# Token order written by ScalarE, a shared kernel mixing, a later gate and a rearranged end in a four-layer vision network on one Trainium2 core

## The chip, the cores and the metric

The kernel runs on one NeuronCore of a Trainium2 chip. The metric is the device time of one execution in microseconds (us). Engines are named as in the profile: PE is TensorE's matmul and PEld its weight load, DVE is VectorE, ACT is ScalarE, POOL is GpSimd, SP is SyncE, which here only issues DMAs. Everything is computed in fp32.

## What is computed

The input is three maps of 256 channels and 48 x 48 pixels. Four layers follow one another; each adds a function of the group-normalised map to the map:

```python
# x: (3, 256, 48, 48); _gn: group norm, 32 groups, no affine part
x = x + layer0(_gn(x))       # 1x1 convolutions and two attention and MLP blocks
x = x + layer1(_gn(x))       # 3x3 convolution, kernel mixed from 8 experts for each map
x = x + layer2(_gn(x))       # plain 3x3 convolution and bias
x = x + layer3(_gn(x))       # Mamba (state-space) block over 2304 tokens of a map

# layer1: the mixed kernel of each map
routing = sigmoid(mean_over_pixels(x) @ routing_ws)             # (3, 8)
ws = einsum('ne,eoihw->noihw', routing, weight)                 # weight (8, 256, 256, 3, 3)

# layer3: tokens in row order, 512 inner channels, 16 states
xn = layer_norm(tokens); x_in, z = split(xn @ in_proj)
u = silu(causal_conv4(x_in)); dt, B, C = projections of u
h = exp(dt * A) * h + dt * B * u            # for each token, channel and state
y = sum over states of h * C + u * D
out = (y * silu(z)) @ out_proj
```

## The kernel before

A map stays in SBUF as 128 partitions (channels) by 2 channel halves (ct) by 2304 pixels. The maps are processed in the order 2, 1, 0. Layer 0 takes the span up to about 1590 us; the change touches there only the count of softmax sums outside a safe range (L841, L842). That count is a product with ones on PE and a copy to `flag`; a flag above zero starts an exact version of the whole network afterwards, which does not happen with this input.

**Layers one and two** are 3x3 convolutions by a one-dimensional fast algorithm along the rows: four neighbouring columns become six transformed columns. So a map lies in four *phases*: pixel (j, n) is column j of group n of four, all n of phase 0 first. Each layer has a *unit* for each map, six units in all; a unit has two halves h of the rows, a half two halves m of the output channels, and these have six products (`products`, L1356) of six matmuls with 288 columns each, which go through five PSUM buffers. ACT copies some of them to SBUF (L1372), DVE turns six products into four phases and adds them to the map. ACT pads the next half (L310) into `xpad`, a pool of one buffer, from which DVE makes the transformed columns `vt`; the moments for the next group norm (`moments`, L1400 and L1407, then PE's group sum L184 and DVE's L186) also use `xpad` for their discarded outputs.

The kernels of the units are made beside other units, by generators that are advanced 13 steps after each output half. `mixed(b)` reads 48 pieces of 128 x 768 (8 experts, 2 ct, 3 taps dx), 384 KB each, and adds each, scaled by its routing weight, to a sum `u`: the first expert on ACT (L273), the others by one DVE operation (L275). Then DVE transforms the sum from three taps to six (L256 to L261), one ct after the other. `mixed(1)` runs beside unit 0 and is needed by unit 1, `mixed(0)` beside unit 1 for unit 2; `mixed(2)` was made earlier. The order of instructions in these units is the scheduler's.

When a unit of layer two is complete, 18 DMAs in all (six for each map, L1460) write the map to the DRAM tensor `xd` in chunks of 384 tokens, phase by phase, in runs of 384 bytes. SP issues those of maps 2 and 1, ACT's queue those of map 0. Beside units 4 and 5, `early_preparation` computes the first steps of layer three for the first chunks.

**Layer three** goes through 18 chunks of 384 tokens (6 for each map). A chunk has 4 blocks m of 128 inner channels, and a block 2 steps (h = 0 and 1) of 8 states; so 8 steps a chunk, 144 in all. A step has 8 parts: one scan on DVE (L1572) with the decays that ACT has made by an exponential in PSUM (L1564, three slots). Before a step its inputs are filled, half by DVE (L1535) and half by POOL (L1539, from `dtur`); after it POOL multiplies the states by C (`times_c`, L1580), and PE adds the states of the step before up in one PSUM tile `ps_y` (`add_states`: a product with D, L1592, and 8 products, L1597; the pool has one buffer). `gate` (L1604) is a DVE product of `ps_y` with the silu of z. A table gives the other work of a chunk to a step's parts, in places MID, LATE and PE_: normalisation and projections of the next chunk, output projection (`project_y`, L1198 and L1202) and store of the last one. All engines' orders are written out by hand there (`keep_order`).

Two stages turn phases into tokens: `group_scale` (L1057) reads the fetched chunk by phases and writes it with a stride of four elements; and `project_y` adds the map to the output with an identity product (L1202) whose input is read with that stride (`in_order`). At the end of the program, behind the last scan, come POOL's `times_c` of the last step, `add_states`, `gate`, and both output projections with their stores.

Of the kernel before, what the change touches and what calls it, by code (L numbers as in the profile page):

```python
# [16 lines left out]
P = 128  # L17
B = 3
# [65 lines left out]
def net(  # L84
# [68 lines left out]

    xd = [dram.tile([P, NCH, CT, CH], F32, name=f"xd{b}", bufs=1) for b in range(B)]
    norm3 = {}
# [106 lines left out]

    def mixed(b, pool):

        u = weights[b] = pool.tile([P, 6, 3, CT, 256], F32, name="u")
        for e in range(EXPERTS):
            for ct in range(CT):
                for dx in range(3):
                    wt = part_of_kernel(we[e], ct, dx)
                    re = route[b][:, e : e + 1]  # L270
                    dst = u[:, dx, :, ct, :]
                    if e == 0:
                        nc.scalar.activation(dst, wt, AF.Copy, scale=re)  # L273
                    else:
                        nc.vector.scalar_tensor_tensor(dst, wt, re, dst, ALU.mult, ALU.add)  # L275
                    yield
        for ct in range(CT):
            kernel_transform(u, ct)
            yield
# [80 lines left out]
    with ExitStack() as l0:  # L360
# [147 lines left out]
        with ExitStack() as p2:  # L508
# [323 lines left out]
            if not exact:  # L832

                ext = small.tile([P, 2], F32, name="ext")
                nc.vector.tensor_reduce(ext[:, 0:1], sums, AX.X, ALU.max)
                nc.vector.tensor_reduce(ext[:, 1:2], sums, AX.X, ALU.min)
                nc.vector.tensor_scalar(ext[:, 0:1], ext[:, 0:1], 1.0 / SUM_MIN, None, ALU.is_gt)
                nc.vector.tensor_scalar(ext[:, 1:2], ext[:, 1:2], 1.0 / SUM_MAX, None, ALU.is_lt)
                nc.vector.tensor_tensor(ext[:, 0:1], ext[:, 0:1], ext[:, 1:2], ALU.add)
                pe = one()  # L840
                nc.tensor.matmul(pe[:1, :1], ext[:, 0:1], ones[:, 0:1], start=True, stop=True)  # L841
                nc.vector.tensor_copy(flag, pe[:1, :1])  # L842

# [95 lines left out]
        for steps in small_steps:  # L939
            at_once(steps)  # L940

    psg = ctx.enter_context(tc.tile_pool(name="psg", bufs=1, space=PSUM))
    rooms, w3v, chunks = {}, {}, {}

# [17 lines left out]
    def w3_rooms():  # L965
# [10 lines left out]
        halves = [t.rearrange("p (t n) -> p t n", t=2) for t in pieces]  # L976
        for name, got in zip(("xp", "xg", "sq", "ot"), (halves[:1], halves[1:2], halves[2:3], halves[3:5])):
            rooms[name] = got
# [54 lines left out]
    def fetch(at):  # L1033
        k = chunks[at] = Chunk()
        k.at = at
        k.b, k.c = todo[at]
        k.before = chunks.get(at - 1)
        k.xp = room(k, "xp")
        nc.sync.dma_start(k.xp, xd[k.b][:, k.c])

# [7 lines left out]

    def in_order(t):

        return t.rearrange("p (j n) -> p n j", j=4)

    def group_scale(k):
        sc, sh = norm3[k.b]
        k.xg = room(k, "xg")
        for ct in range(CT):
            nc.scalar.activation(  # L1057
                k.xg[:, ct, :].rearrange("p (n j) -> p j n", j=4),
                k.xp[:, ct, :].rearrange("p (j n) -> p j n", j=4), AF.Identity,
                bias=sh[:, ct : ct + 1], scale=sc[:, ct : ct + 1],  # L1060
            )
# [133 lines left out]

    def project_y(k, mo):
        for m in range(DI):
            nc.tensor.matmul(  # L1198
                bank[mo], w("out", m * 256 + mo * P, P), k.sz[:, m, :],
                start=m == 0, stop=False,  # L1200
            )
        nc.tensor.matmul(bank[mo], ident, in_order(k.ot[:, mo, :]), start=False, stop=True)  # L1202

    def residual(k):
        k.ot = room(k, "ot")
        nc.sync.dma_start(k.ot, xd[k.b][:, k.c])

# [64 lines left out]
    def early_preparation():  # L1272

        exp_ln_tables()
        fetch(0)
        winx, cwb = x2_rooms()
# [42 lines left out]
        k = chunks[0]  # L1319
        while 1 not in norm3:  # L1320
            yield
# [24 lines left out]
    with ExitStack() as l1:  # L1346
# [42 lines left out]
        units = [(layer, b) for layer in range(2) for b in ORDER]  # L1389
        beside = {0: mixed(1, upools[1]), 1: mixed(0, upools[0]), 2: plain(upools[1])}  # L1390
        halves = [(k, h) for k in range(len(units)) for h in range(2)]
# [21 lines left out]
        def next_norm(layer, b):  # L1413

            last = layer and b == ORDER[-1]
            known = None if last else moments(b)
            for _ in range(5):
                yield
            _, sc, sh = yield from group_norm_steps(b, pss, "s", known=known)
            if layer == 0:  # L1420
                norms[b] = sixth(sc, sh)
            else:
                keep = const.tile([P, 2, CT], F32, name=f"norm3{b}")
                nc.vector.tensor_copy(keep[:, 0, :], sc)
                nc.vector.tensor_copy(keep[:, 1, :], sh)
                norm3[b] = keep[:, 0, :], keep[:, 1, :]
# [8 lines left out]
        def between():  # L1435
            next(pending, None)
            if at_unit >= 4:
                next(early, None)

        vt = first_v  # L1440
        pending = iter(())
        for n, (k, h) in enumerate(halves):
# [7 lines left out]
            for m in range(2):  # L1450
                output(b, h, m, u, vt, v("l2_bias", 0, 2) if layer else None)
                for _ in range(13):
                    next(beside.get(k, iter(())), None)
            vt = ahead
            if layer and h == 1:
                phases = xs[b].rearrange("p t (j n) -> p (t j) n", j=4)

                queue = nc.sync if k + 1 < len(units) else nc.scalar
                for c in range(NCH):
                    queue.dma_start(  # L1460
                        xd[b][:, c].rearrange("p t (j n) -> p (t j) n", j=4),
                        phases[:, :, c * (CH // 4) : (c + 1) * (CH // 4)],
                    )
            if h == 1:
                for _ in pending:
                    pass
                pending = next_norm(layer, b)
                next(pending)
        for _ in pending:
            pass  # L1470
# [9 lines left out]
    with ExitStack() as l3:  # L1480
# [95 lines left out]
        def times_c(s):  # L1576
            at, m, h = steps[s]
            cb = chunks[at].bc[1][:, 2 * h : 2 * h + 2, :].unsqueeze(2)
            hc = scn.tile([P, 2, 4, CH], F32, name="hc")
            nc.gpsimd.tensor_tensor(  # L1580
                hc, tiles[s][:, :, :, 1:], cb.broadcast_to([P, 2, 4, CH]), ALU.mult
# [33 lines left out]
        for s, (at, m, h) in enumerate(steps):  # L1615
            if m == 0 and h == 1 and at + 2 <= last:
                fetch(at + 2)
            for part in range(8):
# [5 lines left out]
                if part % 4 == 1:  # L1624
                    if h == 1 and part == 5 and s >= 3:
                        gate(*steps[s - 3][:2])
                    run(at, j, MID)
                if part % 4 == 3:
                    run(at, j, LATE)
# [16 lines left out]
            if h == 0 and s + 2 < len(steps):  # L1646
                spread_pe(chunks[steps[s + 2][0]], steps[s + 2][1])
        end = len(steps) - 1
        add_states(end)
        gate(*steps[end][:2])  # L1650
        k = chunks[last]
        residual(k)
        for mo in range(2):
            project_y(k, mo)
            store(k, mo)
# [114 lines left out]
```

## Time and profile before

| | us |
|---|---|
| median of 3 runs | 3594.66 (3594.13 to 3596.95) |
| profiled execution, its own time | 3598.05 |
| its span in the profile | 3596.3 |
| units 0 and 1 of the convolutions (1592 to 1774) | 182 |
| unit 2 and layer two (1774 to about 2098) | 324 |
| first scan of layer three | at 2107.64 |
| last scan of layer three ends | at 3570.93 |

Busy time of the whole span: PE 3179.0 us (88%), DVE 3003.0 (84%), ACT 2333.6 (65%), POOL 1440.4 (40%, nearly all of it in layer three). The granted clock was 0.934 in the mean. In the profile a row of the groups gives engine, operation, output and inputs, shapes, how many, then busy time and mean ns of one, then the idle time just before them and what ended it. A product of 128x384 on PE is two records in fp32, one behind the other. In a timeline the columns are start, duration, engine, line, operation, and in brackets the idle time before it and who ended it.

### The profile page before, as it was taken

To read this page: it belongs to the slowest core of one execution; us is meant where nothing else is said; L and a number is where in the kernel's file an instruction comes from. 1 tells how busy PE (TensorE), PEld (TensorE's weight loads), DVE (VectorE), ACT (ScalarE), POOL (GpSimd) and SP (SyncE) were. 2 spreads that over 40 slices of the span, in tenths; PEclk is the share of its full clock that TensorE was granted. 3 is DMA by queue.
4 is the path that set the end of the run, shared out by engine and by line. 5 is a ranking of instruction groups with operands and counts; after the bars stand their busy time and mean duration, and the time that the engine had idled before them with its cause. 6 is when DMAs were issued, how large, how long until landed. Compare 5 with 4: busy or idle time off the path is not lost. (4 is left out here: it accounts for less than half of the span.)

```text
span 3596.3 us, 45582 instructions
## 1 busy us (share of the span) xinstructions
PE 3179.0 (88%) x17154; PEld 1438.0 (40%) x17154; DVE 3003.0 (84%) x3304; ACT 2333.6 (65%) x3477; POOL 1440.4 (40%) x386
## 2 busy tenths in 40 slices
PE   7999999999999999977899987888888888788875
PEld 4323232352322324546677743333333333333331
DVE  4798989959989896479965379999999999999996
ACT  2788787748877875332123447777777777777774
POOL 0000000000000000210000059999999999999998
PEclk9999999999999999988999988889999999888986
DMA  4000000000000001756402234444444444444441
GB/s 181 3 1 1 1 2 1 1 40 1 1 1 1 2 1 60 243 171 219 164 28 58 60 75 116 102 112 106 111 98 111 102 108 101 118 106 107 107 106 36
DMA packets 170648, 266.50 MB, mean 74 GB/s; under 512 B 42849, under 2 KB 137633, under 8 KB 168498
## 3 DMA queue, kind: packets, MB, share of 16 engines
q1 hardware_dynamic: 152082, 243.44, 25.2%
q10 hardware_dynamic: 18336, 20.06, 1.7%
q8 instruction: 136, 2.23, 0.3%
q14 instruction: 94, 0.77, 0.1%
HBM read 216.31 MB, written 46.89 MB: 73 GB/s over the span
## 5 line engine op out<-in xcount | busy, mean ns | idle before, releaser
L610 ACT ACTIVATE pt<-ps_s 128x1024 f32<-128x1024 f32 x972 | 939.0, 1022 | 236.9 <-PE ps_s L606 219.3
L1572 DVE TENSOR_TENSOR_SCAN hs<-ps_da,hs 128x385 f32<-128x385 f32 x1152 | 1012.8, 939 | 63.2 <-ACT ps_da L1564 45.4
L686 DVE TENSOR_TENSOR part<-part,pt 128x2048 f32<-128x2048 f32 x396 | 906.5, 2289 | 79.4 <-ACT pt L610 54.8
L1564 ACT ACTIVATE ps_da<-dtr,u 128x384 f32<-128x384 f32 x1152 | 658.0, 582 | 311.1 <-DVE hs L1572 292.6
L162 POOL TENSOR_TENSOR rstd<-ve,mhalf 128x2 f32<-128x2 f32 (+1 forms) x26 | 17.9, 691 | 1529.1 <-DVE ve L160 1529.1
L606 PE MATMUL ps_s<-q,kt 32*128 32x512 f32 (+1 forms) x4320 | 615.2, 593 | 2.3 <-DVE q L567 0.9
L619 PE MATMUL acc<-pt,vt 128*32 128x512 f32 (+1 forms) x4320 | 522.3, 562 | 8.1 <-DVE o L666 8.0
L1356 PE MATMUL ps_c<-vt,u 128*128 128x288 f32 x1728 | 430.0, 410 | 45.7 <-DVE u L261 45.7
L1580 POOL TENSOR_TENSOR hc<-hs,x 128x3072 f32<-128x3072 f32 x72 | 445.6, 6188 | 37.8 <-PE ps_g L1155 13.4
L1580 POOL TENSOR_TENSOR hc<-hs,bc 128x3072 f32<-128x3072 f32 x72 | 444.1, 6169 | 37.7 <-DVE hs L1572 14.1
L1109 PE MATMUL ps_g<-u 128*128 128x384 f32 x1152 | 389.2, 493 | 3.1 <-ACT u L1118 3.1
L1356 PEld LDWEIGHTS ps_c<-vt,u 128*128 128x128 f32 x1728 | 330.3, 192 | 140.1 <-issue 34.8
L606 PEld LDWEIGHTS ps_s<-q,kt 32*128 32x128 f32 x4320 | 220.0, 183 | 388.5 <-issue 227.1
L1109 PEld LDWEIGHTS ps_g<-u 128*128 128x128 f32 x1152 | 215.0, 190 | 174.5 <-issue 14.0
L1597 PE MATMUL ps_y<-hc,u 128*32 128x384 f32 x2304 | 246.1, 550 | 30.7 <-POOL hc L1580 27.4
L1539 POOL TENSOR_TENSOR hs<-dtur,x 128x1536 f32<-128x1536 f32 x72 | 247.9, 3443 | 17.4 <-DMA dtur<-dtud 8.8
L1539 POOL TENSOR_TENSOR hs<-dtur,bc 128x1536 f32<-128x1536 f32 x72 | 248.5, 3451 | 6.5 <-ACT ps_g L1087 2.4
L619 PEld LDWEIGHTS acc<-pt,vt 128*32 128x32 f32 x4320 | 95.7, 108 | 363.8 <-issue 328.1
L1155 PE MATMUL ps_g<-wconv,u 17*128 17x384 f32 x144 | 79.2, 684 | 97.2 <-ACT x L1176 97.2
L1372 ACT COPY cb<-ps_c 128x288 f32<-128x288 f32 x48 | 19.0, 396 | 219.1 <-PE ps_c L1356 200.7
L1067 PE MATMUL ps_g<-wconv,u 128*128 128x384 f32 x144 | 87.5, 780 | 67.0 <-ACT x L1176 66.6
L1597 PEld LDWEIGHTS ps_y<-hc,u 128*32 128x32 f32 x2304 | 64.6, 118 | 201.9 <-issue 151.0
(236 smaller groups left out, 3517.1 us busy)
## 6 DMA issues: line engine op xcount, KB each, us to landing
wconv<-in_we SPq DMA_DIRECT2D x144, 384.0 KB, 4.3
dtr<-dtd SPq DMA_DIRECT2D x288, 192.0 KB, 3.8
dtur<-dtud SPq DMA_DIRECT2D x288, 96.0 KB, 4.1
wconv<-xd SPq DMA_DIRECT2D x36, 384.0 KB, 4.4
x<-bcd SPq DMA_DIRECT2D x72, 192.0 KB, 5.8
dtd<-x SPq DMA_DIRECT2D x36, 384.0 KB, 2.4
bc<-bcd SPq DMA_DIRECT2D x72, 192.0 KB, 5.5
yc<-ycat ACTq DMA_DIRECT2D x18, 576.0 KB, 4.7
```

What stands on the lines that cost most here:

```text
L606: nc.tensor.matmul(s[:, j, cols], kt[r, mt * P : (mt + 1) * P], q[r, :n], start=True, stop=True,)
L610: nc.scalar.activation(p[:, h0 : h0 + 2, :], s, AF.Exp)
L619: nc.tensor.matmul(acc[h * HD : (h + 1) * HD, :n], vt[:, mt, g * P + h * HD : g * P + (h + 1) * HD], p[:, h, cols], start=mt == 0, stop=mt ...
L686: nc.vector.tensor_tensor(part, first_p if group == 1 else part, p, ALU.add)
L1067: nc.tensor.matmul(bank[to], w3v["less"][:, int(to != ct), :], k.xg[:, ct, :], start=ct == 0, stop=ct == CT - 1,)
L1109: nc.tensor.matmul(bank[m % 2], w3v["wtap"][:, tap, ct, m * P : (m + 1) * P], k.xn[:, ct, tap : tap + CH], start=tap == 0 and ct == 0, sto ...
L1356: nc.tensor.matmul(pc[:, :HN], u[:, i, dy, ct, m * P : (m + 1) * P], vt[:, i, ct, dy * TW : dy * TW + HN], start=ct == 0 and dy == 0, stop ...
L1539: nc.gpsimd.tensor_tensor(hs[:, :, 2:4, 1:], k.rows[m][1].unsqueeze(1).broadcast_to([P, 2, 2, CH]), bb, ALU.mult,)
L1564: nc.scalar.activation(slots[n % 3][:, 1 : CH + 1], chunks[at].rows[m][0][:, q, :], AF.Exp, scale=amat[:, col : col + 1],)
L1572: nc.vector.tensor_tensor_scan(b, slots[(8 * s + part) % 3][:, : CH + 1], b, 0.0, ALU.mult, ALU.add)
L1580: nc.gpsimd.tensor_tensor(hc, tiles[s][:, :, :, 1:], cb.broadcast_to([P, 2, 4, CH]), ALU.mult)
L1597: nc.tensor.matmul(k.y_ps[32 * q : 32 * q + 32, :CH], fold, hc[:, g, q, :], start=False, stop=h == 1 and g == 1,)
```

## The change

1. *Token order.* `xd` becomes 2304 tokens in order for each channel half. `store_tokens` lets ACT write half a map in token order (12 copies of 128x1152 in all, with a stride of four elements) into an `xpad` buffer, or for the last half into a `vt` buffer, and one DMA of 1.18 MB stores it; it is called in the middle of the half that follows. `group_scale` then works in place on contiguous tokens, `project_y`'s identity product reads contiguously and comes first. `early_preparation` waits for the stores it reads, and `next_norm` yields nine times in place of five.
2. *Kernel mixing.* In `mixed(1)` and `mixed(0)` one piece of the six of each expert (second ct, third dx) is no longer added by ACT and DVE: ACT writes the routing weight times the identity into `each`, PE multiplies the piece with it in two products of 384 columns, which add up over the experts in two PSUM banks, and after the last expert ACT copies the sums to `u` in four pieces.
3. *Gate.* `gate` stands behind part 7's scan and no longer behind part 5's.
4. *Count.* The product with ones and the copy to `flag` are issued behind the small steps of the convolution part.
5. *End.* The last step's `times_c` is two DVE products of 128x1536; the identity products and three of the four products of each output projection stand before the last `add_states`.

```diff
@@ -151,7 +151,7 @@
     ycat = [dram.tile([P, 3, N], F32, name=f"ycat{b}", bufs=1) for b in range(B)]
-    xd = [dram.tile([P, NCH, CT, CH], F32, name=f"xd{b}", bufs=1) for b in range(B)]
+    xd = [dram.tile([P, CT, N], F32, name=f"xd{b}", bufs=1) for b in range(B)]
     norm3 = {}
@@ -260,7 +260,10 @@
...
         nc.vector.tensor_tensor(g1, t, g1, ALU.add)
-    def mixed(b, pool):
+    def mixed(b, pool, shared=False):
         u = weights[b] = pool.tile([P, 6, 3, CT, 256], F32, name="u")
@@ -269,7 +272,23 @@
...
                     dst = u[:, dx, :, ct, :]
-                    if e == 0:
+                    if shared and ct == CT - 1 and dx == 2:
+                        flat = wt.rearrange("p y o -> p (y o)")
+                        each = tmp.tile([P, P], F32, name="each")
+                        nc.scalar.activation(each, ident, AF.Copy, scale=re)
+                        for j in range(2):
+                            nc.tensor.matmul(
+                                bank[j], each, flat[:, j * 384 : (j + 1) * 384],
+                                start=e == 0, stop=e == EXPERTS - 1,
+                            )
+                        if e == EXPERTS - 1:
+                            for y, o, n in ((0, 0, 256), (1, 0, 128), (1, 128, 128), (2, 0, 256)):
+                                at = y * 256 + o
+                                j = at // 384
+                                nc.scalar.copy(
+                                    dst[:, y, o : o + n], bank[j][:, at - 384 * j : at - 384 * j + n]
+                                )
+                    elif e == 0:
                         nc.scalar.activation(dst, wt, AF.Copy, scale=re)
@@ -837,9 +856,6 @@
...
                 nc.vector.tensor_tensor(ext[:, 0:1], ext[:, 0:1], ext[:, 1:2], ALU.add)
-                pe = one()
-                nc.tensor.matmul(pe[:1, :1], ext[:, 0:1], ones[:, 0:1], start=True, stop=True)
-                nc.vector.tensor_copy(flag, pe[:1, :1])
         early.close()
@@ -938,12 +954,16 @@
...
             at_once(steps)
+        if not exact:
+            pe = one()
+            nc.tensor.matmul(pe[:1, :1], ext[:, 0:1], ones[:, 0:1], start=True, stop=True)
+            nc.vector.tensor_copy(flag, pe[:1, :1])
     psg = ctx.enter_context(tc.tile_pool(name="psg", bufs=1, space=PSUM))
-    rooms, w3v, chunks = {}, {}, {}
+    rooms, w3v, chunks, stored = {}, {}, {}, set()
     def room(k, name):
@@ -974,7 +994,7 @@
...
         halves = [t.rearrange("p (t n) -> p t n", t=2) for t in pieces]
-        for name, got in zip(("xp", "xg", "sq", "ot"), (halves[:1], halves[1:2], halves[2:3], halves[3:5])):
+        for name, got in zip(("xg", "sq", "ot"), (halves[:2], halves[2:3], halves[3:5])):
             rooms[name] = got
@@ -1035,8 +1055,8 @@
...
         k.before = chunks.get(at - 1)
-        k.xp = room(k, "xp")
-        nc.sync.dma_start(k.xp, xd[k.b][:, k.c])
+        k.xg = room(k, "xg")
+        nc.sync.dma_start(k.xg, xd[k.b][:, :, k.c * CH : (k.c + 1) * CH])
     class Chunk:
@@ -1046,17 +1066,11 @@
-    def in_order(t):
-        return t.rearrange("p (j n) -> p n j", j=4)
     def group_scale(k):
         sc, sh = norm3[k.b]
-        k.xg = room(k, "xg")
         for ct in range(CT):
             nc.scalar.activation(
-                k.xg[:, ct, :].rearrange("p (n j) -> p j n", j=4),
-                k.xp[:, ct, :].rearrange("p (j n) -> p j n", j=4), AF.Identity,
+                k.xg[:, ct, :], k.xg[:, ct, :], AF.Identity,
                 bias=sh[:, ct : ct + 1], scale=sc[:, ct : ct + 1],
@@ -1193,17 +1207,18 @@
...
         nc.scalar.copy(k.sz[:, m, :], bank[j])
-    def project_y(k, mo):
-        for m in range(DI):
+    def project_y(k, mo, lo=0, hi=DI):
+        if lo == 0:
+            nc.tensor.matmul(bank[mo], ident, k.ot[:, mo, :], start=True, stop=False)
+        for m in range(lo, hi):
             nc.tensor.matmul(
                 bank[mo], w("out", m * 256 + mo * P, P), k.sz[:, m, :],
-                start=m == 0, stop=False,
+                start=False, stop=m == DI - 1,
             )
-        nc.tensor.matmul(bank[mo], ident, in_order(k.ot[:, mo, :]), start=False, stop=True)
     def residual(k):
         k.ot = room(k, "ot")
-        nc.sync.dma_start(k.ot, xd[k.b][:, k.c])
+        nc.sync.dma_start(k.ot, xd[k.b][:, :, k.c * CH : (k.c + 1) * CH])
     def store(k, mo):
@@ -1272,6 +1287,8 @@
...
         exp_ln_tables()
+        while (2, 1) not in stored:
+            yield
         fetch(0)
@@ -1317,7 +1334,7 @@
...
         k = chunks[0]
-        while 1 not in norm3:
+        while 1 not in norm3 or (1, 1) not in stored:
             yield
@@ -1387,7 +1404,7 @@
         units = [(layer, b) for layer in range(2) for b in ORDER]
-        beside = {0: mixed(1, upools[1]), 1: mixed(0, upools[0]), 2: plain(upools[1])}
+        beside = {0: mixed(1, upools[1], True), 1: mixed(0, upools[0], True), 2: plain(upools[1])}
         halves = [(k, h) for k in range(len(units)) for h in range(2)]
@@ -1414,7 +1431,7 @@
...
             known = None if last else moments(b)
-            for _ in range(5):
+            for _ in range(9):
                 yield
@@ -1437,8 +1454,30 @@
...
                 next(early, None)
+        def store_tokens(b, h):
+            last = (b, h) == (ORDER[-1], 1)
+            if last:
+                t = vp.tile([P, 6, CT, (HR + 2) * TW], F32, name="vt")
+                t = t.rearrange("p i t n -> p (i t n)")
+            else:
+                t = pad.tile([P, 4, CT * (HR + 2) * PW + 2], F32, name="xpad")
+                t = t.rearrange("p j n -> p (j n)")
+            t = t[:, : CT * 4 * HN].rearrange("p (t n) -> p t n", t=CT)
+            for ct in range(CT):
+                nc.scalar.copy(
+                    t[:, ct, :].rearrange("p (n j) -> p j n", j=4),
+                    xs[b][:, ct, :].rearrange("p (j n) -> p j n", j=4)[
+                        :, :, h * HN : (h + 1) * HN
+                    ],
+                )
+            queue = nc.scalar if last else nc.sync
+            queue.dma_start(xd[b][:, :, h * 4 * HN : (h + 1) * 4 * HN], t)
+            stored.add((b, h))
         vt = first_v
-        pending = iter(())
+        behind, pending = None, iter(())
         for n, (k, h) in enumerate(halves):
@@ -1451,21 +1490,18 @@
...
                     next(beside.get(k, iter(())), None)
+                if m == 0 and behind is not None:
+                    store_tokens(*behind)
+                    behind = None
             vt = ahead
-            if layer and h == 1:
-                phases = xs[b].rearrange("p t (j n) -> p (t j) n", j=4)
-                queue = nc.sync if k + 1 < len(units) else nc.scalar
-                for c in range(NCH):
-                    queue.dma_start(
-                        xd[b][:, c].rearrange("p t (j n) -> p (t j) n", j=4),
-                        phases[:, :, c * (CH // 4) : (c + 1) * (CH // 4)],
-                    )
+            if layer:
+                behind = b, h
             if h == 1:
...
                 next(pending)
+        store_tokens(*behind)
         for _ in pending:
@@ -1577,6 +1613,15 @@
...
             hc = scn.tile([P, 2, 4, CH], F32, name="hc")
+            if s == len(steps) - 1:
+                for g in range(2):
+                    nc.vector.tensor_tensor(
+                        hc[:, g], tiles[s][:, g, :, 1:],
+                        cb[:, g].broadcast_to([P, 4, CH]), ALU.mult,
+                    )
+                tiles[s] = hc
+                return
             nc.gpsimd.tensor_tensor(
@@ -1622,9 +1667,9 @@
...
                 if part % 4 == 1:
-                    if h == 1 and part == 5 and s >= 3:
-                        gate(*steps[s - 3][:2])
                     run(at, j, MID)
+                if h == 1 and part == 7 and s >= 3:
+                    gate(*steps[s - 3][:2])
                 if part % 4 == 3:
@@ -1645,13 +1690,16 @@
...
         end = len(steps) - 1
-        add_states(end)
-        gate(*steps[end][:2])
         k = chunks[last]
...
         for mo in range(2):
-            project_y(k, mo)
+            project_y(k, mo, 0, DI - 1)
+        add_states(end)
+        gate(*steps[end][:2])
+        for mo in range(2):
+            project_y(k, mo, DI - 1, DI)
             store(k, mo)
```

## The prediction

> **What bounds the kernel now.** I read the page's busy shares and slices first: no engine is the bound of the whole (PE 88%, DVE 84%, ACT 65%, POOL 40%), so the span was cut into stages. The table by stage (core, window, its length, then busy time of PE, PEld, DVE, ACT, POOL, the granted clock, DMA share, GB/s):
>
> ```profile
> 1592.00:1685.00 93.00, 73.85 (x298) 57.17 (x298) 91.82 (x154) 26.61 (x32) 2.23 (x7) 0.89 0.64 219
> 1685.00:1774.00 89.00, 72.51 (x292) 56.44 (x292) 88.24 (x144) 17.79 (x22) 2.79 (x7) 0.90 0.60 205
> ...
> 1845.00:2098.00 253.00, 252.48 (x1001) 187.76 (x999) 130.67 (x290) 82.11 (x109) 5.83 (x19) 1.00 0.21 54
> ...
> 2113.00:3571.00 1458.00, 1178.89 (x4832) 529.09 (x4832) 1355.22 (x1514) 1087.72 (x2062) 1365.58 (x288) 0.87 0.43 103
> ```
>
> Units 0 and 1 of the convolutions are bound by DVE, which mixes the next unit's kernel (99% busy). Layer two is bound by PE (252.48 of 253). The state-space layer, 1458 of 3596 us, has DVE and POOL both at 93%: 81 us for a chunk, of which POOL's own work is 8 x (3.45 + 6.18) = 77.0. Next the waits: DVE's in the state-space layer, and PE's in the convolutions (us in total, times, longest).
>
> ```profile
> DVE hs L1572 <- ACT ps_da L1564: 42.3, 52, 1.1
> DVE wconv L1091 <- ACT ps_g L1087: 19.0, 16, 1.3
> DVE x L1604 <- PE ps_y L1597: 11.3, 16, 1.1
> DVE sz L1604 <- PE ps_y L1597: 11.3, 16, 1.1
> ```
>
> ```profile
> PE ps_c L1356 <- DVE u L261: 45.7, 3, 19.2
> PE ps_gm L184 <- ACT xpad L1400: 9.2, 2, 4.9
> ```
>
> The gate (L1604) loses 22.6 us in 32 waits. The timeline of DVE in one chunk shows which gates: the first and second of four, in the steps where PE has no pause.
>
> ```profile
> 2862.15 0.56 DVE L1604 TENSOR_TENSOR x<-ps_y,x 128x384 f32<-128x384 f32 x1 [0.36 <-PE ps_y L1597]
> ...
> 2881.10 0.56 DVE L1604 TENSOR_TENSOR sz<-ps_y,sz 128x384 f32<-128x384 f32 x1 [1.05 <-PE ps_y L1597]
> ```
>
> Sizes of what is edited, from the groups:
>
> ```profile
> L275 DVE SCALAR_TENSOR_TENSOR u<-wconv,route,u 128x768 f32<-128x768 f32 x126 | 120.6, 1009 | 0.6 <-DMA wconv<-in_we 0.4
> L1057 ACT ACTIVATE wconv<-wconv,norm 128x384 f32<-128x384 f32 x36 | 34.3, 1052 | 3.5 <-DVE norm L1425 3.5
> L1202 PE MATMUL ps_g<-wconv,ident 128*128 128x384 f32 x72 | 52.8, 822 | 0.0
> ```
>
> And the end, after the last scan at 3570.93 (called E below): the timeline.
>
> ```profile
> 3566.86 12.27 POOL L1580 TENSOR_TENSOR hc<-hs,bc 128x3072 f32<-128x3072 f32 x2
> ...
> 3581.69 0.56 DVE L1604 TENSOR_TENSOR sz<-ps_y,sz 128x384 f32<-128x384 f32 x1 [10.76 <-PE ps_y L1597]
> ...
> 3590.35 0.48 ACT L1209 COPY wconv<-ps_g 128x384 f32<-128x384 f32 x1 [3.41 <-PE ps_g L1202]
> ```
>
> POOL's product of the last step (6.1 us, to 3579.13) precedes PE's last sums, and both output projections stand behind the gate.
>
> **What the Trainium skill says.** *SBUF — State Buffer*, "Specifications (TRN2)", says SBUF has 16-byte lines and full speed needs at least two accesses to a line. The trace agrees: L1057 writes at a 16-byte stride and takes 1052 ns, L1118 on as many contiguous elements 563; L1202 reads at that stride, 822 ns, L1198 contiguously 495. *ScalarE: Activation LUTs*, "What ACT_TABLE_LOAD costs", gives 186 ns + 0.833 ns an element for an activation with immediates (1146 ns for 1152 elements); used below. *DMA: Bandwidth & Descriptors*, "Specifications", puts the least transfer at line rate at 512 bytes; the present token stores use 384-byte runs and land in 2.8 to 7.5 us (median 4.6), as the loads of longer runs do, so no penalty is plain here. *GPSIMD Engine Reference*, "1. Specifications", says POOL shares SBUF interfaces with DVE instructions that have two SBUF inputs; it bears on the end, and no row before shows it alone.
>
> **The change part by part.** Sums are against the profiled execution, 3598.05 us (span 3596.3), which is 3.4 above the median.
>
> *Flag.* PE waited 6.15 us at the flag's product, but its next product waits for an ACT result of 1411.2, reached after a table load. Worth 0; cover gone, at most 6.
>
> *Kernel mixing (units 0 and 1).* Each map loses 7 L275 products of DVE, 0.93 us apart in a row: -6.5, and one ACT scaling of 0.94. Added: on PE 16 products 128x384 at 0.69 (L1198: four in 2.76) = 11.0; on ACT 8 small scalings (about 0.4) and 4 copies from PSUM (about 0.45). PE's gaps, 19.2 and 16.5, hold the 11.0. But PE works in order: the last expert's pair stands behind nearly all of the unit's own products, and behind it the four copies, the second moment on ACT, the group sum L184, DVE's reading of it, then the transform of the second channel half (4 x 0.95). Unit 0: products ended at 1665.6; +11.0 for the pairs, +1.8 copies, +1.2 moment, +1.0 sum, +3.8 transform = 1684.4, against 1685.3: -0.9, where DVE alone would give -6.5. Unit 1: 1757.3 + 18.8 = 1776.1 against 1774.3: +1.8. Together **+1**. Ends: -13 if the chain is shorter than DVE; +20 if weight loads, whose buffers now come free on PE and not DVE, come late.
>
> *Token order in layer two.* 12 ACT copies 128x1152 with strided writes: 1146 ns plus 1152 x (1052 - 563)/384 = 1.5 us, so 2.6 each (3.2 by scaling L1057); 32 us on ACT, which has 171 us free in that window. A pair holds ACT for 5.3 us; behind it wait the PSUM copies L1372. A product is six matmuls of 0.41, 2.5 us; five buffers give some 7 us before PE stops. The copies use the one xpad buffer, so the next half's padding waits for ACT and for a store of 1.18 MB. Away go SP's 12 and ACT's 6 issues (0.36 to 2.6 us each), which hold nobody. I take **+2** (-1 to +8). At the change to the state-space layer the last products come 2.75 us earlier (only the last z projection stands behind them), while on ACT a copy pair stands before the store, and that store (1.18 MB beside the first dtr and dtur loads; the window before has DMA 90% busy) takes from them: **0** (-3 to +6), the preparation that now waits for the stores included.
>
> *Token order in the state-space layer.* L1057 gets shorter by 0.49 x 2 a chunk; ACT is 75% busy and waits for PE and DVE after it: 0. L1202's pair goes from 1.47 to about 0.7, twice a chunk, on PE ahead of the second gate: it helps the next step.
>
> *The gate.* Two scans and the gap, 1.73 us, later. The longest wait was 1.1; the first gate's sum is ready at 2862.15 and would be asked for at about 2863.5, the second ready at 2881.10, asked for at about 2881.4 once both stalls are gone, with L1202's saving beyond that. The wait goes in both. What is behind the gate: ps_y has one buffer, and PE starts the next sum (L1592) 4.6 to 7.8 us after the gates' ends in three of four cases of a chunk, 1.8 in the other: no room is lost. After that POOL is next late, but 81.0 - 1.4 is still above its 77.0. Of 22.6 I take nine tenths: **-20** (0 to -24).
>
> *The end.* DVE's two products 128x1536, as L1535: 1.73 each, E+3.5. PE: sums of the last step but one E+4.9, eight products of the projection (6.6) E+11.5, sums E+14.1, gate E+14.9, one product each, last copy from E+17.0, and 5.95 from there as before: E+23.0 against E+25.4: **-2.4** (-1 to -5; if POOL's running product holds DVE, 2 us of it go).
>
> Sum: 0 + 1 + 2 + 0 - 20 - 2.4 = -19.4; 3598.05 - 19.4 - 3.4 = **3575**.
>
> **Rivals.**
> A. *The wait moves.* PE is without a pause in the first four steps; if it falls behind with DVE, or if POOL's late products (its waits sum to 98 us) become DVE's waits, the state-space layer keeps its length: 0 for the gate, 3595. For: PE's continuous run, margin 0.3 us. Against: only the second gate is thin, and DVE waited for POOL 2.4 us in all.
> B. *Slower: weight loads wait for PE.* In units 0 and 1 a piece's buffer that PE reads comes free only when in-order PE has passed its own products. If seven loads in each unit come one landing (4.3 us) late, DVE idles 14 x 4.3 = 60, less the 13 saved: +47, so about 3621. It decides from about seven such loads on (30 us, against -22 elsewhere). For: DMA is 60% busy there and DVE at 99%, with no slack. Against: DVE waited 0.4 us for loads, and the paired pieces are one in six.
> C. *All of DVE's relief is kept.* -13 for the mixing, rest as above: 3561.
> D. *The change does not do what it says.* The scheduler places the convolutions' instructions; if the pairs drift to the unit's end each unit loses about 5: 3585.
>
> **How the numbers follow.** Forecast 0.46, A 0.18, B 0.20, C 0.12, D 0.04. About 2 in 10 lie outside 3556 (C with a full gate gain) to 3610 (A with layer two's and the transition's upper ends, or B with nine late loads). A measurement can tell about 0.2%, 7.2 us, from no change. Faster: forecast, C and D, 0.62, A is "same", 0.18; B is slower, 0.20.
>
> **What would show it.** Right: no wait of the gate for ps_y; chunks near 80 us; unit 1 starting about 93 us after unit 0, unit 2 about 91 after that, PE then without a gap to the last unit; ACT's copies at 2.6; the last instruction 23 us after the last scan. Wrong: gate waits that stay or turn up at L1572 or at POOL; DVE idle for weight loads in units 0 and 1; PE gaps over 8 us in layer two; a first scan over 10 us after the last convolution product.

## The result, and the profile after

The changed kernel takes 3550.16 us (median of 4, 3548.09 to 3551.30), the one before 3594.39 in the same comparison: ratio 0.9876, 95% interval 0.9859 to 0.9893. It is 44 us faster; 19.4 had been forecast, and the range ended at 3556. The profiled execution of the changed kernel took 3550.73, its span is 3548.9, which is 47.4 less than the span before. In the new numbering the scan is L1608, its decay L1600, the gate L1649, PE's sums L1637 and L1642, DVE's mixing product L294, and PE's pairs of mixing products L280.

The same stages of both profiled executions, from their timelines:

| stage, us | before | after | difference | forecast |
|---|---|---|---|---|
| up to the start of unit 0 | 1592.3 | 1589.3 | -3.0 | 0 |
| units 0 and 1 | 182.0 | 175.0 | -7.0 | +1 |
| unit 2's start to the second group of scans | 338.4 | 343.5 | +5.1 | +2 |
| from there to the last scan's end | 1458.2 | 1420.0 | -38.1 | -20 |
| behind the last scan | 25.4 | 21.0 | -4.4 | -2.4 |

The first row is not the change: in the profiles of the experiments below, where little or nothing ahead of unit 0 differs, it starts anywhere from 1585.3 to 1593.6. So stages are compared by their lengths. These vary too where nothing in the stage was edited: layer three is 1455.2 with the mixing alone, against 1458.2 before, and the stretch from unit 2 to the second group of scans lies between 338.4 and 339.8 in the six profiles without the token order and between 341.1 and 345.2 in the seven with all of it and the mixing. In these two stages a difference of 3 us is therefore not a finding by itself.

The table by stage for the changed kernel (window, length, busy time of PE, PEld, DVE, ACT, POOL, clock, DMA share, GB/s):

```profile
1589.32:1676.67 87.35, 84.84 (x332) 63.39 (x333) 82.27 (x144) 17.88 (x30) 1.52 (x4) 0.97 0.64 216
1676.67:1764.35 87.68, 83.05 (x324) 62.01 (x324) 83.65 (x139) 28.21 (x43) 2.07 (x7) 0.98 0.63 215
1764.35:2094.58 330.23, 325.49 (x1286) 245.47 (x1287) 186.39 (x403) 118.80 (x138) 7.68 (x26) 0.98 0.15 46
2107.86:3527.90 1420.04, 1152.52 (x4830) 526.66 (x4830) 1350.56 (x1514) 1076.85 (x2062) 1363.73 (x288) 0.88 0.44 106
```

Units 0 and 1: PE went from 74 to 85 us of work, the pairs' 11, and DVE gave up 9.5 and 4.6. Layer three: DVE does the same 1514 instructions, in 1350.6 us in place of 1355.5, and its idle time fell from 102.7 to 69.5 us. DVE's waits in that window:

```profile
DVE hs L1608 <- ACT ps_da L1600: 34.1, 46, 1.1
DVE wconv L1105 <- ACT ps_g L1101: 16.7, 15, 1.3
DVE hs L1608 <- POOL hs L1575: 4.4, 1, 4.4
```

The gate is gone from the list (22.6 before), and the decays' waits are 34.1 where they were 42.3. PE's waits from unit 0 to the end of layer two:

```profile
PE ps_c L1373 <- DVE u L261: 21.9, 2, 19.1
PE ps_gv L193 <- DVE gd L190: 4.7, 1, 4.7
PE ps_gm L184 <- ACT xpad L1417: 3.2, 2, 2.4
```

Unit 1's wait for its kernel is gone from the list, and unit 2 waits 2.9 us (21.9 is 19.1 ahead of unit 0, as before, and this). New is the stop of 4.7 us in layer two. Sizes, from the groups:

```profile
L294 DVE SCALAR_TENSOR_TENSOR u<-wconv,route,u 128x768 f32<-128x768 f32 x112 | 108.2, 1009 | 6.9 <-DMA wconv<-in_we 6.9
...
L1212 PE MATMUL ps_g<-wconv,ident 128*128 128x384 f32 x72 | 31.1, 513 | 0.0
...
L1072 ACT ACTIVATE wconv<-wconv,norm 128x384 f32<-128x384 f32 x36 | 23.4, 693 | 11.3 <-DVE norm L1442 11.3
...
L1469 ACT COPY xpad<-x 128x1152 f32<-128x1152 f32 x10 | 22.5, 2312 | 17.7 <-DVE x L1403 6.4 <-DMA xd<-xpad 4.3 <-DVE we L348 4.2
...
L1619 DVE TENSOR_TENSOR hc<-hs,bc 128x1536 f32<-128x1536 f32 x2 | 5.3, 2692 | 0.0
```

The identity product fell from 822 to 513 ns; the group scale from 1052 to 693, not to 563; a token copy takes 2.31 us (2.6 estimated). The end, from the timeline:

```profile
3528.34 5.31 DVE L1619 TENSOR_TENSOR hc<-hs,bc 128x1536 f32<-128x1536 f32 x2
...
3538.49 1.50 PE L1642 MATMUL ps_y<-hc,u 128*32 128x384 f32 x16
3540.06 0.56 DVE L1649 TENSOR_TENSOR sz<-ps_y,sz 128x384 f32<-128x384 f32 x1 [6.41 <-PE ps_y L1642]
```

The last sums now stand behind PE's own partial projections; DVE's products are done 4.8 us earlier, at 3533.65.

### The profile page after: what moved, and what is told of

Read it like the earlier page. It is cut to its first block, busy times and chain, and to the rows that moved or that the text cites. A ratio compares the mean times of both kernels' runs of the same rounds, so it can differ in the third digit from the quotient of the medians.

```text
span 3548.9 us, 45802 instructions
## 1 busy us (share of the span) xinstructions
PE 3174.5 (89%) x17218; PEld 1449.6 (41%) x17218; DVE 2992.2 (84%) x3292; ACT 2350.6 (66%) x3511; POOL 1431.5 (40%) x385
## 3 DMA queue, kind: packets, MB, share of 16 engines
q1 hardware_dynamic: 145570, 244.62, 25.4%
## 5 line engine op out<-in xcount | busy, mean ns | idle before, releaser
L1608 DVE TENSOR_TENSOR_SCAN hs<-ps_da,hs 128x385 f32<-128x385 f32 x1152 | 1004.9, 938 | 54.0 <-ACT ps_da L1600 34.8
L1600 ACT ACTIVATE ps_da<-dtr,u 128x384 f32<-128x384 f32 x1152 | 657.9, 582 | 292.3 <-DVE hs L1608 269.8
L1373 PE MATMUL ps_c<-vt,u 128*128 128x288 f32 x1728 | 434.5, 412 | 22.0 <-DVE u L261 21.9
L1123 PEld LDWEIGHTS ps_g<-u 128*128 128x128 f32 x1152 | 214.9, 190 | 174.9 <-ACT ps_da L1600 18.7
L1642 PE MATMUL ps_y<-hc,u 128*32 128x384 f32 x2304 | 244.6, 547 | 14.8 <-POOL hc L1625 14.5
L1642 PEld LDWEIGHTS ps_y<-hc,u 128*32 128x32 f32 x2304 | 64.3, 117 | 173.8 <-issue 139.8
```

Of the source, the lines that this page charges most:

```text
L1123: nc.tensor.matmul(bank[m % 2], w3v["wtap"][:, tap, ct, m * P : (m + 1) * P], k.xn[:, ct, tap : tap + CH], start=tap == 0 and ct == 0, sto ...
L1373: nc.tensor.matmul(pc[:, :HN], u[:, i, dy, ct, m * P : (m + 1) * P], vt[:, i, ct, dy * TW : dy * TW + HN], start=ct == 0 and dy == 0, stop ...
L1600: nc.scalar.activation(slots[n % 3][:, 1 : CH + 1], chunks[at].rows[m][0][:, q, :], AF.Exp, scale=amat[:, col : col + 1],)
L1608: nc.vector.tensor_tensor_scan(b, slots[(8 * s + part) % 3][:, : CH + 1], b, 0.0, ALU.mult, ALU.add)
L1642: nc.tensor.matmul(k.y_ps[32 * q : 32 * q + 32, :CH], fold, hc[:, g, q, :], start=False, stop=h == 1 and g == 1,)
```

## The experiments

Each ratio is to the kernel before, in the same comparison. "Layer three" is the fourth row of the table above.

**The parts alone.** First the gate's place.

```diff
-                    if h == 1 and part == 5 and s >= 3:
-                        gate(*steps[s - 3][:2])
                     run(at, j, MID)
+                if h == 1 and part == 7 and s >= 3:
+                    gate(*steps[s - 3][:2])
```

> The kernel before with the gate behind part 7's scan and nothing else. Layer three got 38 us shorter in the changed kernel (from the second group of scans to the last one), where 22.6 us of gate waits were there to win. Theory 1: nearly all of it is the gate's; a stop costs DVE about 0.09 us more than its idle time, because the neighbouring scans no longer overlap, and the decays' waits shrink with it. Then this kernel is 26 to 34 us faster (about 3564). Theory 2: the gate gives its 22.6 us or less and the rest comes from the token order (shorter work on ACT and PE in each chunk). Then it is 15 to 23 us faster (3572 to 3579).

3566.84 us, ratio 0.9917 (0.9903 to 0.9930): 30 us. Layer three is 1426.8, 31.4 shorter, more than the waits there were to win. The gate's 22.6 are gone, and the decays' waits are 5.0 less than before:

```profile
DVE hs L1572 <- ACT ps_da L1564: 37.3, 60, 1.0
```

So theory 1's size holds; its reason had to be tested by itself (below). Second, the token order alone (`xd`, `store_tokens`, `group_scale`, `project_y`, the waits for the stores):

> The kernel before with the token order alone: ScalarE's copies and stores in layer two, contiguous normalisation and identity product in layer three; mixing, gate place, count and end as before. Theory 1: the convolution part gets 2 to 6 us longer and layer three at most 6 us shorter, so the total is within 5 us of before. Theory 2: layer three gets 12 to 15 us shorter with the gate where it was, for PE reaches the gate's sum sooner by the identity product's saving, so the total is 8 to 12 us less.

3589.05, ratio 0.9978 (0.9970 to 0.9986), 8 us less. Layer three is 1448.0, 10.2 shorter, between what the two theories had said (at most 6, and 12 to 15), and DVE's waits there say where: the gate's are 12.1 in place of 22.6.

```profile
DVE hs L1588 <- ACT ps_da L1580: 45.0, 50, 1.0
DVE wconv L1085 <- ACT ps_g L1081: 18.1, 16, 1.2
DVE sz L1620 <- PE ps_y L1613: 6.1, 16, 0.4
DVE x L1620 <- PE ps_y L1613: 6.0, 16, 0.4
```

That is theory 2's account, with a smaller size: PE, relieved of the strided identity product, reaches the gate's sum sooner. The stretch with layer two is 340.6, 2.2 longer. Third, the mixing alone (`shared=True` for two maps):

> The kernel before with TensorE's share of the mixing alone. In the changed kernel unit 0 took 87.4 us (before 93.0) and unit 1 87.7 (before 89.0). If the mixing alone does this, the unit starts move by -5.6 and -6.9 and the total is 7 us less (3587). If part of it comes from the token order or the count (their changed places in the scheduler's order), units 0 and 1 together gain under 4 us here. The prediction's chain behind the last pair would give 1 us more than before.

3589.45, ratio 0.9978 (0.9968 to 0.9988), 7 us less. Unit 0 takes 86.4 us, unit 1 87.2: the mixing alone does it. Fourth, the end alone:

> The kernel before with the shorter end alone (the identity product still reads with a stride). The changed kernel ended 21.0 us after its last scan, the one before 25.4. If the end alone does this, less the two strided identity products (0.65 us each longer, but ahead of the last sums), the total is 4.4 us less, 3590; the prediction's own sum was 2.4.

3593.69, ratio 0.9992 (0.9983 to 1.0000); its profile ends 22.0 us after the last scan, before 25.4. The interval reaches "no change", but the length of that stage shows 3.4.

**Do the parts add up?** The changed kernel with the gate back at part 5:

> The changed kernel with the gate back behind part 5's scan. Alone, the gate's place gave 30 us and the token order 8 us; all parts alone sum to 48, together they gave 44 to 47. Theory 1: the token order's part in layer three is a shorter wait of the gate (12.1 us of gate waits were left with it alone, of 22.6), so with the gate back 11 to 13 us of gate waits return, and with the silu behind it some 7 more: 3571 (20 to 22 slower than the changed kernel). Theory 2: the parts add up: 30 slower, 3580.

3580.66, ratio 0.9956 (0.9943 to 0.9970), 29 slower than the changed kernel by the ratios. Layer three is 1448.0, as with the token order alone, 27.9 longer than with the gate late. Of these the gate's waits are only 12.0; the decays' waits are 44.9 in place of 34.1. So the gate's place is worth far more than its own waits, and theory 1 falls.

**What of the token order counts in layer three.** With the late gate it still gives 6.7 us there (1426.8 to 1420.0). Two ways it could: ACT's scale or PE's identity product.

```diff
-                k.xg[:, ct, :], k.xg[:, ct, :], AF.Identity,
+                k.xg[:, ct, :].rearrange("p (n j) -> p j n", j=4),
+                k.xp[:, ct, :].rearrange("p (j n) -> p j n", j=4), AF.Identity,
```

> The changed kernel, with ScalarE's group scale in layer three again reading by phases from one buffer and writing another with a stride of four elements, as before (tokens then stand in a wrong order: the computation of layer three is changed, not its amount). Layer three of the changed kernel is 6.7 us shorter than with the gate moved alone. Theory 1: ACT's 0.36 us for each of two copies a chunk lie beside other work, so nothing measurable comes back (under 3 us). Theory 2: ACT's time before the chain centre, mean, inverse root counts: 5 to 7 us come back, in DVE's waits for the inverse root and the decays.

3548.91, ratio 0.9867 (0.9852 to 0.9883); layer three 1417.6: nothing comes back. ACT's time there is covered, as the prediction had it.

```diff
-            nc.tensor.matmul(bank[mo], ident, k.ot[:, mo, :], start=True, stop=False)
+            nc.tensor.matmul(bank[mo], ident, k.ot[:, mo, :].rearrange("p (j n) -> p n j", j=4), start=True, stop=False)
```

> The changed kernel, with the identity product of the output projection reading with a stride again (so the map is added in a wrong order; the amount of work is that of before). Theory 1: PE's 0.66 us for each pair, twice a chunk, made only the second gate late; with the gate at its new place it is hidden, except for the second gate's thin margin: under 3 us come back. Theory 2: it is the source of the 6.7 us: 5 to 8 us come back, half a us a chunk, as gate waits.

3561.94, ratio 0.9898 (0.9883 to 0.9914), 8 us slower by the ratios. The interval overlaps that of the changed kernel, but every run (3558.2 to 3565.4) is slower than every run of the version with the strided scale (3544.6 to 3550.8), which was measured in the same comparison. Layer three is 1427.7, which is all of the 6.7 and a little more, and the end 2.8 us longer. But no gate wait comes back. The decays' waits rise from 34.1 us in 46 stops to 38.4 in 60, and the wait for the inverse root from 16.7 to 18.7. ACT's waits for the finished output, in the changed kernel and then in this one, show where it starts:

```profile
ACT wconv L1224 <- PE ps_g L1214: 7.8, 16, 0.5
ACT wconv L1224 <- PE ps_g L1214: 18.4, 16, 1.2
```

ACT's timeline of the kernel with the gate alone, which has the same strided identity product, shows the road:

```profile
2859.66 0.48 ACT L1209 COPY wconv<-ps_g 128x384 f32<-128x384 f32 x1 [1.14 <-PE ps_g L1202]
2860.03 0.59 ACT L1564 ACTIVATE ps_da<-dtr,u 128x384 f32<-128x384 f32 x1
```

and DVE's, in the same step, the fourth of a chunk:

```profile
2860.66 0.96 DVE L1572 TENSOR_TENSOR_SCAN hs<-ps_da,hs 128x385 f32<-128x385 f32 x1 [0.21 <-ACT ps_da L1564]
```

ACT's copy of the finished output waits 1.14 us for the identity product, the decays stand behind it in ACT's order, and the eighth scan is late. In the changed kernel the eight scans of that step follow one another without a pause (6.91 us from 2850.83). So a slow product on PE, whose result nobody needs soon, reached DVE through ACT's order.

**Why the gate's place gives more than its waits.** In the fourth step of a chunk (the recorded expectations call it the third) the table puts the silu of u at part 7: two table loads and the silu, 4 us in which ACT makes no decay. From the kernel with the gate alone:

```profile
2862.26 1.28 ACT L1123 ACT_TABLE_LOAD   x1
2863.55 1.48 ACT L1123 ACTIVATE x<-x 128x1536 f32<-128x1536 f32 x1
2865.05 1.28 ACT L227 ACT_TABLE_LOAD   x1
```

The three decays in PSUM last for 2.6, so DVE stalls. With the gate at part 7, DVE does it in that stall, which gets shorter by the gate's time. Here is the scan behind this silu before, and with the gate alone:

```profile
2970.74 4.36 DVE L1572 TENSOR_TENSOR_SCAN hs<-ps_da,hs 128x385 f32<-128x385 f32 x5 [1.04 <-ACT ps_da L1564]
...
2867.07 4.36 DVE L1572 TENSOR_TENSOR_SCAN hs<-ps_da,hs 128x385 f32<-128x385 f32 x5 [0.57 <-ACT ps_da L1564]
```

The test puts a copy of the same size in the silu's place in both kernels, so that the two table loads go and 1.46 us of ACT's work stay:

```diff
-        (7, LATE, 1, lambda k: silu(k.u)),
+        (7, LATE, 1, lambda k: nc.scalar.copy(k.u, k.u)),
```

> The kernel before, with the silu of u in layer three replaced by a copy of the same size, so without its two table loads of 1.28 us (u is then not passed through the silu). To be read with the next run: what the gate's place is worth without the stall behind this silu. Here the scan's wait behind that silu (about 1.04 us in a chunk) goes: 14 to 20 us less than before.

3577.68, ratio 0.9945 (0.9932 to 0.9959), as expected; layer three is 1438.4, 19.8 shorter than before.

> The same without the silu of u, and with the gate behind part 7. Theory 1: the gate's move gave more than its 22.6 us of waits since the third step's gate (0.45 us between its neighbours) now runs while ACT is held by the silu of u for 4 us, where DVE stalled anyway: the stall fell from 1.04 to 0.57 us in 17 chunks, 8 us. Without that silu the move is then worth the waits and the lost overlap of 32 stops only: 25 us less than the run above. Theory 2: the excess has nothing to do with the silu: 30 us less than the run above.

3556.37, ratio 0.9886 (0.9870 to 0.9901). The gate's place is worth 21.3 us by the medians and 19.2 in layer three, with the silu 31.4. That is less than both theories said (25 and 30), and theory 2 is out. So 12 us of the 31 need the silu. The shorter stall is worth about 8 of them (0.47 us in each of 17 chunks); the other 4 were not taken apart. Without the silu the move is worth a little less than its waits, since some of them come back as the decays' (26.0 us in 29 stops, then 27.7 in 46). The same reasoning says what else should help: let the other silu, that of z, also run beside a gate.

```diff
-        (1, LATE, 0, lambda k: silu(k.sz)),
+        (3, LATE, 0, lambda k: silu(k.sz)),
```

> The changed kernel, with the silu of z behind part 7 of step 1 and no longer behind part 7 of step 0. Step 1 has a gate behind its part 7, step 0 has none. Theory 1 (a gate behind a silu costs DVE nothing): the scan's wait behind the silu of z falls from 1.04 to 0.57 us in 17 chunks, 8 us less in layer three than the changed kernel, 3542. Theory 2: the wait behind the silu depends on when PE lets ACT go, and stays at 1.04: no difference, or a loss of some us where the u stages come later on ACT.

3542.54, ratio 0.9851 (0.9836 to 0.9866). Layer three is 1412.1, 8.0 shorter than in the changed kernel, the figure of theory 1; the decays' waits are 20.5 in place of 34.1. Its interval overlaps that of the changed kernel's ratio. But the last version below, whose layer three is the changed kernel's (1420.3), was measured in the same comparison, and its runs (3550.2 to 3556.7) are all slower than these (3540.7 to 3546.2). The later silu of z is the fastest version run. In DVE's timeline the first line is the scan behind the silu of z (1.04 us of stall in the changed kernel; why it fell to 0.30 and not to 0.57 was not looked into), the second the one behind the silu of u:

```profile
2836.06 4.36 DVE L1608 TENSOR_TENSOR_SCAN hs<-ps_da,hs 128x385 f32<-128x385 f32 x5 [0.30 <-ACT ps_da L1600]
...
2854.65 4.36 DVE L1608 TENSOR_TENSOR_SCAN hs<-ps_da,hs 128x385 f32<-128x385 f32 x5 [0.57 <-ACT ps_da L1600]
```

**A move that only looks alike.** DVE also waits 16.7 us for the inverse root; its product can stand two scans later too, with the stage that reads it behind it.

```diff
-        (14, LATE, 2, normalise),
-        (15, MID, 2, tokens),
+        (15, MID, 2, normalise),
+        (15, LATE, 2, tokens),
```

> The changed kernel with one more move of the same kind: the product with the inverse root (16.7 us of DVE's waits for ACT, 15 of them, one in nearly every chunk) stands behind part 5's scan of the last step and no longer behind the scan two before, and the stage that reads it two parts later. If such a wait is won by standing two scans (1.73 us) later, as the gate's was, 16.7 us and 0.09 for each of 15 stops go: 18 us less than the changed kernel, 3532. Rival: the decays' waits of that step grow by what is saved, for ACT then does the tokens' stage just ahead of the next step: 0 to 6 us.

3559.23, ratio 0.9895 (0.9880 to 0.9910): 7 us slower than the changed kernel by the ratios. Here too the intervals overlap, but all runs (3556.8 to 3562.0) are slower than those of the strided scale in the same comparison, and layer three is 8.1 us longer (1428.2). The inverse root's 16.7 are gone, and the decays' waits rise from 34.1 to 59.1, which is more than the rival had allowed:

```profile
2822.24 0.96 DVE L1608 TENSOR_TENSOR_SCAN hs<-ps_da,hs 128x385 f32<-128x385 f32 x1 [1.52 <-ACT ps_da L1600]
2823.11 0.93 DVE L1105 TENSOR_TENSOR wconv<-wconv,ps_g 128x768 f32<-128x768 f32 x1
```

The inverse root is ACT's, and in ACT's order the next decays stand behind it (they start at 2821.61, behind a gap of 2.2 us without a decay). So DVE, which no longer waits at the product, meets ACT's delay at the scan before it. That the gate could be moved because it waited for PE and not for ACT is the likely reason for the difference; it was not tested by itself.

**The stop in layer two.**

```diff
-            queue = nc.scalar if last else nc.sync
+            queue = nc.scalar
```

> The changed kernel, with all six token stores issued from ACT's queue. In its trace PE stops once in layer two, 4.7 us at 1943.6, for a group sum; DVE is late there, as it waited 6.2 us for the taps' weights, whose loads stand on SP behind the third store, which waited for ACT's copies until 1925.3. Theory 1: SP's order is the cause; with the store on ACT's queue the loads are issued some us earlier, both waits go, and the stretch from unit 2's start to the second group of scans gets 3 to 5 us shorter: 3546. Theory 2: the loads wait for buffers, not for SP, or the DMA engines are busy with the store: no difference.

3554.91, ratio 0.9884 (0.9869 to 0.9899): no difference (the stretch is 343.6 in place of 343.5), and PE's stop is 6.2 us. Counted from unit 2's start, the loads were issued at 161.0 us in place of 161.6 (148.7 before), and still behind ACT's copies: the profile names them as what the first load waits for, since the loads fill the SBUF room of map 2, which the copies read last. So theory 2 holds in the part that says that the loads wait for their room, and SP's order is not the cause. That PE stops because of these loads is read from the trace alone, where DVE waits 6.2 us for them and then comes late to the group sum; no run moved them clear of the copies.

## Why the prediction was wrong

Leaving out the first row of the table, the stages are 25 us shorter in all than forecast: 18 of them lie in layer three, 8 in units 0 and 1, 2 at the end, and the stretch with layer two took 3 back.

*The gate* (-20 taken, -24 as the end of its range): the wait did go in both places, and the second gate fitted. The step that failed is "Of 22.6 I take nine tenths", which took the waits for the whole prize. Alone it measured -31.4 in layer three: the 22.6, 5.0 of the decays' waits, 2.6 of DVE's busy time (1355.5 to 1352.9), and 1.2 in small waits. What was not asked is where the gate's own 0.45 us would lie: in the fourth step it went into a stall that was there anyway, and without the silu that makes this stall the move was worth only 19.2. The busy time fits the smaller number of stops: a scan behind a stop is listed with 0.96 us, eight in a row with 6.91, so 0.85 for each one that follows without a pause. POOL did not become the bound: 1363.7 of 1420.0.

*Token order in layer three* (0): right for ACT's scale, wrong for the identity product. The step that failed is "it helps the next step", which left it without a number; it is worth 7 us with the late gate, on the road through ACT's copy, and 10 with the early one.

*Kernel mixing* (+1, from a chain of 18.8 us behind the unit's own products): -8.4 alone in units 0 and 1. The 11.0 of the chain that are the pairs were right: the last pair ended 84.4 us after unit 0's start (1673.69), and 84.3 had been summed. The step that failed is the 7.8 behind it, of which only 3.0 passed before unit 1 began at 1676.67. The four copies took 0.96 us and not 1.8; the group sum L184 waits for the first moment only, and comes ahead of the second moment and of most of the copies' time; and unit 1 begins as soon as one half of its kernel is transformed, while DVE makes the other. The timeline of the kernel before shows the last point too, for there unit 1 starts at 1685.32, between the ends of the two halves:

```profile
1684.27 0.94 DVE L261 TENSOR_TENSOR u<-wconv,u 128x768 f32<-128x768 f32 x1
...
1686.73 0.94 DVE L261 TENSOR_TENSOR u<-wconv,u 128x768 f32<-128x768 f32 x1
```

The relief was kept in unit 0 (-6.6 of 6.5) and mostly lost in unit 1 (-1.8). In the changed kernel DVE waits for weight loads 6.9 us in 9 waits over both units (0.4 before), 3.3 of it in unit 1: rival B on a small scale, where 60 in 14 had been priced.

*Layer two and the transition* (+2): +2.2 with the token order alone, +5.1 in the changed kernel, inside the bounds. The named wait, ACT's copies ahead of PSUM copies, did not stop PE. The stop came from the room of map 2, a wait the prediction did not list. The 5.1 are this stop, 2.3 us more of PE's busy time for the same 1326 products (335.1 to 337.4; the granted clock was 1.00 and then 0.99), and 2.0 less of PE's other idle time. Why the busy time rose stays open, and the difference between 2.2 and 5.1 is within what this stretch varies (341.1 to 345.2 in the changed kernel and its variants).

*The end* (-2.4): -4.4, -3.4 alone. DVE's two products took 5.31 us and not 3.46, and they were not alike: the first took 3.64, the second 1.75. The first ran beside POOL's last product, which ended at 3530.36, the second behind it:

```profile
3524.14 6.22 POOL L1625 TENSOR_TENSOR hc<-hs,bc 128x3072 f32<-128x3072 f32 x1
...
3528.34 3.64 DVE L1619 TENSOR_TENSOR hc<-hs,bc 128x1536 f32<-128x1536 f32 x1
```

So the 1.73 taken from L1535 was right for the product alone, and the 1.9 above it are what the prediction had named as "if POOL's running product holds DVE, 2 us of it go". All eight kernels with this end show the same: 3.57 to 3.80 us, then 1.74 or 1.75. That agrees with what the Trainium skill says (*GPSIMD Engine Reference*, "1. Specifications"), that POOL shares its SBUF interfaces with DVE instructions that have two SBUF inputs, as these have. The delay cost nothing, since PE was busy until 3538.49. PE's six partial products with the two identity products took 5.4 us where 6.6 had been taken, and the last sums 1.50 for 2.6.

*The count* (0): PE now waits 6.03 us at 1403 for ACT in place of 6.15 for DVE. Right.

Of the rivals, A (the wait moves) did not come true for the gate, but it did for the inverse root; of C, 8.4 of its 13 us came true.

## What to carry to other kernels

The length of a wait is not the whole price of an instruction's place: look also at whether the engine would stand idle at the new place anyway. Here the gate's work cost DVE nothing behind the silu of u, and its full time ahead of it. Ask also which engine releases the wait: where the same engine feeds the next instruction, as ACT does with the inverse root and the decays, the later place moved the stall and made it longer. And look at each of a group's instructions, not only at their mean: the mean of 2.69 us of DVE's last two products hid one of 3.64 and one of 1.75.

## What had not been expected of the hardware

The group scale took 692 ns in place on contiguous tokens and 1052 with the stride, so the stride cost 0.36 us. The prediction had compared it with another activation of 128x384 (L1118, 563 ns, from PSUM) and took 0.49; with 692 its own sum for a token copy gives 2.2 us, and 2.31 were measured. DVE's product of 128x1536 with both operands in SBUF took 3.64 us while POOL's product ran, and 1.75 behind it.
